# Filters made earlier and Strassen factors kept on chip in the first image, and the last projection shared out differently, in a YOLO-style attention block on one core

## The chip, the cores and the metric

The kernel runs on one core of a Trainium2 chip. The metric is device time in microseconds of one execution. Every run has a granted TensorE clock in its record (1.0 is full speed).

## The reference, cut to what matters

```python
B, C1, C2, N, F, HEADS = 8, 512, 512, 2, 32, 4     # 8 images of 32x32, C = 256, fp32
# per image (the tail is told in comments, the functions are the reference's own)
# y = cbs(x, cv1_w): 1x1, 512 -> 512, cut into two halves of 256 channels, y0 and y1
# for i in 0, 1:     3x3 convolution (256 -> 256) + silu, qkv 1x1,
#                    attention of 4 heads over 1024 positions, then m_cv2 (1x1),
#                    silu, plus the residual -> y2, y3
# out = cbs(concat(y0, y1, y2, y3), cv2_w) + x
def cbs(x, w, p, pad):
    return jax.nn.silu(bn_eval(conv2d(x, w, pad), p))

def bot_attention(x, qkv_w, rw, rh):
    ...
    r = (rw + rh).reshape(1, HEADS, HD, hw)
    logits = jnp.einsum('bhdi,bhdj->bhij', q, k + r) * HD ** (-0.5)
    a = jax.nn.softmax(logits, axis=-1)
    out = jnp.einsum('bhij,bhdj->bhdi', a, v)
```

## The kernel before

The kernel takes the images one after the other. Three of its devices matter here.

**Convolution by transformed filters.** A 3x3 convolution is done on transformed inputs and transformed filters (`u`), in three *pairs*. For image 0 VectorE makes the filters (`make_u`) from raw weights and stores each pair (1 MB) to memory; images 1 to 7 only load them. The ring that holds filters has five slots of 1 MB.

```python
    def make(n, oc, i):
        us[oc, i] = u = new_u("u_new")
        for k in range(NM):
            last = make_u(i, u[:, k], raws[n, oc, k])
        nc.gpsimd.dma_start(u_dram[n][oc][i], u)
        return last
...
        def u_of(n):
            def of(oc):
                if b == 0 and (oc, 0) not in us:     # second half of the channels, image 0
                    for k in range(NM):
                        if (n, oc, k) not in raws:
                            raws[n, oc, k] = load_raw(n, oc, k, "kv"[k])
                    with tc.issue_after(last.ins):
                        for i in range(PAIRS):
                            make(n, oc, i)
```

**Strassen for the last projection (cv2) of images 0 to 6.** Four sums of weight blocks are made once, in image 0, stored, and read back by every image, image 0 too. `make_ws` stores them, `load_ws` reads four half-MB sums and three source blocks. Image 7 uses plain products, with parts of them done early (`parts`, `begun`) so that its end is short.

**Attention in four groups** (two channel blocks by two halves of positions). While a group runs, the one before it is finished: a row of softmax sums goes to memory and comes back over 128 partitions, VectorE takes reciprocals (`rc`), which go to memory and back as a spread tile (`rs`), and `scale` multiplies. The accumulator of attention times V (`av_ps`) has one buffer; it is released by the add in `times_v`. An instruction on VectorE that waits holds up those queued behind it (shown below, L574 behind L640).

```python
                if j0 + PAIR == NJ:                 # times_v, last pair of a group
                    nc.scalar.copy(dst, av[:, 0])
                    nc.vector.tensor_tensor(dst, av[:, 1], dst, ALU.add)    # releases av_ps
...
            for i in range(len(pairs) + 1):
                if i < len(pairs):
                    added = logits(pairs[i])
                    g, at_q = divmod(i, NQ)
                    with tc.issue_after(added.ins):
                        if at_q == NQ - 2 and g > 0:
                            rss[g - 1] = spread(g - 1, s_drams[g - 1])     # rc, r_dram, rs
                        if at_q == 0 and g > 1:
                            scale(g - 2, rss.pop(g - 2))                   # waits for rs
```

The end of image 7 takes output pieces of 128 x 512 through two `t` buffers (add the early part, silu, add the residual `x_res`, store).

## Time and profile before

| | us |
|---|---|
| time before, median of the first three runs | 2406.1 |
| the profiled run (span; clock 0.995) | 2407.3 |
| image 0, from its first convolution to image 1's | 316.5 |
| ... its first attention / second convolution / second attention | 58.2 / 28.9 / 68.3 |
| images 1 to 6, each | 292.5 to 294.1 |
| image 7, last m2 (the 1x1 convolution after the attention) to the last add | 28.0 |

Stages are timed from the start of their first matmul on TensorE to that of the next stage; the second convolution is timed to the end of its last matmul, and qkv from there, since the two overlap by 0.16 us. The timeline of TensorE after the second convolution of image 0 (columns: start, length, engine, line, operation, output<-inputs; in brackets the idle time before it and who ended it, where there was any):

```profile
216.64 3.60 PE L303 MATMUL ps<-z,qkv_sb 128*128 128x512 f32 x8
220.07 1.03 PE L489 MATMUL v_ps<-qkv_sb,z 128*128 128x256 f32 x4
221.13 3.70 PE L303 MATMUL ps<-z,qkv_sb 128*128 128x512 f32 x8
```

And VectorE at the very end:

```profile
2398.14 1.35 DVE L928 TENSOR_TENSOR t<-ps,part 128x512 f32<-128x512 f32 x2 [3.90 <-PE ps L303]
```

VectorE waits 3.90 us for TensorE's products, so TensorE is what the end of the kernel before hangs on.

### The profile page before, as it was taken

The numbers are of one execution on the slowest core, as the hardware profiler recorded it, in microseconds if no ns is written. First come the engines' busy times: TensorE is split into PE (matmuls) and PEld (weight loads), VectorE is DVE, ScalarE is ACT, GpSimd is POOL, SyncE is SP. The second block draws the span as 40 slices with busy tenths as digits, with TensorE's granted clock in tenths as the row PEclk, the third lists the DMA queues.
The fourth block names the chain that finished last, engine by engine and source line by source line (L and its number), as shares of the span: only waits on it lengthen the run. The fifth ranks groups of instructions, "written<-read, shape, count | busy, mean of one in ns | idle before, by whom it ended". The sixth has DMA issues, their size and how long they took to land.

```text
span 2407.3 us, 35330 instructions
## 1 busy us (share of the span) xinstructions
PE 2358.4 (98%) x14514; PEld 1180.1 (49%) x14514; DVE 1589.4 (66%) x2549; ACT 925.7 (38%) x1230; POOL 85.6 (4%) x301
## 2 busy tenths in 40 slices
PE   7999899999999999999999999999999999999998
PEld 4536246363453635536364463645536364463633
DVE  8867675666766667666676656866566765666654
ACT  1442423526244251443425344252432525325252
POOL 1000000000100001000010000100001000000001
PEclk9999999999999999999999999999999999999999
DMA  7312325030340304203051021601107020150202
GB/s 244 116 34 97 132 78 207 15 114 15 114 167 15 114 15 168 117 10 114 22 217 62 28 96 32 260 13 66 59 28 262 11 99 25 47 199 15 71 10 68
DMA packets 90376, 215.19 MB, mean 89 GB/s; under 512 B 27616, under 2 KB 48288, under 8 KB 77664
## 3 DMA queue, kind: packets, MB, share of 16 engines
q1 hardware_dynamic: 79008, 165.15, 19.9%
q0 software_dynamic: 11200, 47.72, 5.1%
q8 instruction: 116, 1.90, 0.3%
q14 instruction: 52, 0.43, 0.1%
HBM read 180.85 MB, written 31.98 MB: 88 GB/s over the span
## 4 chain that ended last, share of the span: by engine, by line
PE 92%; DVE 4%; DMA 3%; ACT 0%; issue 0%; SPq 0%; POOL 0%; ACTq 0%; DVEq 0%
PE ps L303 20%; PE av_ps L550 18%; PE l_ps L524 18%; PE c_ps L740 12%; PE c L795 8%; PE c_new L795 6%; PE m_ps L761 5%; PE v_ps L489 5%; DMA u<-u 1%; PE s_ps L568 1%; PE s_ps L586 1%; DMA rs<-r_dram 0%; DMA s_dram<-s_row 0%; DVE acc L536 0%; DVE v_in L362 0%
## 5 line engine op out<-in xcount | busy, mean ns | idle before, releaser
L528 ACT ACTIVATE pt<-l_ps 128x1024 f32<-128x1024 f32 x512 | 494.9, 1023 | 309.7 <-PE l_ps L524 308.3
L536 DVE TENSOR_TENSOR acc<-acc,pt 128x1024 f32<-128x1024 f32 x384 | 469.5, 1223 | 122.8 <-ACT pt L528 99.1
L550 PE MATMUL av_ps<-pt,vT 64*64 64x512 f32 x4096 | 486.8, 593 | 3.7 <-DVE ao L558 3.7
L524 PE MATMUL l_ps<-q,kr 64*64 64x512 f32 x4096 | 484.8, 591 | 0.0
L740 PE MATMUL c_ps<-v_in,u 128*128 128x128 f32 x2688 | 304.3, 275 | 7.0 <-DVE v_in L362 4.0
L740 PEld LDWEIGHTS c_ps<-v_in,u 128*128 128x128 f32 x2688 | 303.0, 192 | 14.9 <-issue 9.4
L524 PEld LDWEIGHTS l_ps<-q,kr 64*64 64x64 f32 x4096 | 153.8, 133 | 279.9 <-issue 268.3
L550 PEld LDWEIGHTS av_ps<-pt,vT 64*64 64x64 f32 x4096 | 152.1, 133 | 281.1 <-issue 228.1
L303 PE MATMUL ps<-z,qkv_sb 128*128 128x512 f32 x512 | 229.3, 595 | 1.3 <-ACT z L289 0.9
L303 PE MATMUL ps<-x,w 128*128 128x512 f32 x512 | 227.0, 600 | 2.2 <-DVE x L439 2.2
L534 DVE TENSOR_TENSOR acc<-pt 128x1024 f32<-128x1024 f32 x64 | 78.4, 1225 | 134.7 <-ACT pt L528 134.7
L303 PEld LDWEIGHTS ps<-x,w 128*128 128x128 f32 x512 | 96.8, 192 | 130.3 <-issue 127.0
L477 DVE TENSOR_TENSOR kr<-ps,rw_sb 128x512 f32<-128x512 f32 x64 | 41.2, 686 | 176.5 <-PE ps L303 176.5
L303 PEld LDWEIGHTS ps<-z,qkv_sb 128*128 128x128 f32 x512 | 94.7, 190 | 108.1 <-issue 91.8
L795 PE MATMUL c_new<-t_in,ws 128*128 128x512 f32 x336 | 145.3, 592 | 0.0
L369 ACT COPY m<-c_ps 128x256 f32<-128x256 f32 x96 | 35.5, 369 | 234.9 <-PE c_ps L740 226.6
L489 PE MATMUL v_ps<-qkv_sb,z 128*128 128x256 f32 x512 | 115.7, 379 | 0.0
L761 PE MATMUL m_ps<-ao,m_sb 128*128 128x512 f32 x256 | 112.5, 592 | 0.0
L489 PEld LDWEIGHTS v_ps<-qkv_sb,z 128*128 128x128 f32 x512 | 97.3, 190 | 26.9 <-issue 15.3
L795 PEld LDWEIGHTS c_new<-t_in,ws 128*128 128x128 f32 x336 | 63.8, 190 | 80.4 <-issue 77.0
L289 ACT ACTIVATE m_kept<-m_kept,bh,sh 128x512 f32<-128x512 f32 x42 | 31.9, 806 | 146.0 <-DVE m_kept L879 86.3
L624 DVE TENSOR_TENSOR ao<-ao,rs 128x512 f32<-128x512 f32 x64 | 44.1, 689 | 63.3 <-DMA rs<-r_dram 62.8
(153 smaller groups left out, 2130.7 us busy)
## 6 DMA issues: line engine op xcount, KB each, us to landing
u<-u SPq DMA_DIRECT2D x84, 1024.0 KB
x<-in_x_dram SPq DMA_DIRECT2D x32, 512.0 KB
x_res<-in_x_dram POOLq DMA_DIRECT2D x28, 512.0 KB, 9.1
ws<-s SPq DMA_DIRECT2D x28, 512.0 KB
out_dram<-m_kept POOLq DMA_DIRECT2D x28, 512.0 KB, 7.5
w<-in_cv_w_dram SPq DMA_DIRECT2D x13, 1024.0 KB
u<-u_new POOLq DMA_DIRECT2D x12, 1024.0 KB, 5.9
rs<-r_dram SPq DMA_DIRECT2D x96, 128.0 KB
```

The costliest lines, as they stand in the source:

```text
L303: nc.tensor.matmul(ps[:, half, :], w_of(k), rhs_of(k, half), start=(k == begin), stop=(k == end))
L477: nc.vector.tensor_tensor(dst, img(ps[:, half, :]), rw, ALU.add)
L489: nc.tensor.matmul(ps[:, at, :], z[:, k, ts(j0 + at, P)], qkv_sb[:, n, k, 2 * C : 3 * C], start=(k == 0), stop=(k == NM - 1),)
L524: nc.tensor.matmul(ps[kh * HD : (kh + 1) * HD, hd, :], kr[r, c, o : o + HD], q[r, c, ts(half, HALF)], start=True, stop=True,)
L528: exp = nc.scalar.activation(pt[:, i], ps, AF.Exp, scale=SCALE)
L534: return nc.vector.tensor_tensor(accs[g], pt[:, 0], pt[:, 1], ALU.add)
L536: ins = nc.vector.tensor_tensor(accs[g], accs[g], pt[:, i], ALU.add)
L550: nc.tensor.matmul(avs[g][hd * HD : (hd + 1) * HD, kh, :], vT[r, j, o : o + HD], pt[r, i, hd, :], start=(j == 0), stop=(j == NJ - 1),)
L624: nc.vector.tensor_tensor(dst, dst, rs, ALU.mult)
L740: nc.tensor.matmul(ps[:, row, col, :], us[i][:, k, row, SLOT[col], :], vs[i][:, k, row, col, :], start=(k == 0), stop=(k == NM - 1),)
L761: nc.tensor.matmul(pss[oc][:, half, :], m2_sb[:, n, k, ts(oc, P)], ao[:, k, ts(half, HALF)], start=(k == 0), stop=(k == NM - 1),)
L795: nc.tensor.matmul(ps[:, o, :], w[:, k, ts(o, P)], rhs[part][:, c, :], start=(k == 0 and not onto), stop=(k == KB - 1), skip_group_check=onto,
```

## The change

Three parts. Part 1: in image 0 the Strassen sums that VectorE has just made are handed to Strassen where they lie, with the source blocks; they are stored for the other images, but not read back. Part 2: of the three filter pairs of the second convolution's second half, pair 2 is made in group 0 of the first attention (stored, dropped and loaded again) and pair 0 in groups 1 and 2 (kept); pair 1 alone stays beside the convolution. Part 3: image 7's early products are shared out differently: four more are begun in the gap before its last convolution, and the last block is ordered half by half.

```diff
 def make_ws(w2):
-        return [nc.gpsimd.dma_start(dst, w) for w, dst in zip(sums, s_dram2)][-1]
+        last = [nc.gpsimd.dma_start(dst, w) for w, dst in zip(sums, s_dram2)][-1]
+        return last, (a11, s1, a12, s4, s2, s3, a22)
 ...
-                three = s.strassen(b, load_ws(), y0, y1)
+                three = s.strassen(b, ws or load_ws(), y0, y1)
 ...                                                       # part 2
-                    with tc.issue_after(last.ins):
-                        for i in range(PAIRS):
-                            make(n, oc, i)
+                        with tc.issue_after(last.ins):
+                            make(n, oc, [1])
 ...
+            if b == 0:                                     # ahead(), first attention
+                if g == 0:
+                    raws[1, 1, 0], raws[1, 1, 1] = load_raws_y0(1, 1)
+                    make(1, 1, [2])
+                    del us[1, 2]
+                elif g <= NM:
+                    make(1, 1, [0], [g - 1])
 ...                                                       # part 3
-            for oc in range(3, NO):
-                parts[oc] = s.cv2_part(w1, (y0, y1), oc)
+            parts[3] = s.cv2_part(w1, (y0, y1), 3)
+            parts[0] = s.cv2_part(w1, (y0, y1), 0, range(NM))
 ...
-                begun = s.cv2_products(w2, (y0, y1, y2), 0, range(N * NM))
+                ks = range(NM, (1 + N) * NM)
+                begun[0] = s.cv2_products(w2, (y0, y1, y2), 0, ks, ends=(ks[0], (2 + N) * NM - 1))
 ...
-                s.cv2_products(w2, (y0, y1, y2), 0, range(N * NM, (1 + N) * NM), begun)
+                ks = range(2 * NM, (1 + N) * NM)
+                begun[1] = ps_av.tile([P, NH, HALF], F32, tag="av", name="ps")
+                s.cv2_products(w2, (y0, y1, y2), 1, ks, begun[1], (ks[0], (2 + N) * NM - 1))
 ...                                                       # in cv2(): the last block by halves
+                        ps = cv2_products(w2, ys, oc, ks, ends=(ks[0], ks[-1]), by_half=oc == NO - 1)
```

Left out: `make` in its form by pairs and channel groups, and the loading of raw filters in two tiles (`load_raws_y0`).

More of the change, by code (lines that the diff above doesn't have):

```diff
@@ L123, in load_w2, with rows_of_raw @@
         return ws
+    def rows_of_raw(raw):
+        rows = raw.rearrange("p (r c) o -> p r c o", c=3)
+        return rows[:, 0::2], rows[:, 1]
     def load_raw(n, oc, k, tag, bufs=1):
@@ L127, in load_raw, with load_raws_y0 @@
         nc.sync.dma_start(raw, m_cv1_w[n, ts(k, P), :, ts(oc, P)])
-        return raw
+        return rows_of_raw(raw)
+    def load_raws_y0(n, oc):
+        raw = act.tile([P, 16, P], F32, tag="y0", name="raw", bufs=2)
+        mid = act.tile([P, 3, P], F32, tag="xr", name="raw_mid", bufs=2)
+        src = m_cv1_w[n, P : 2 * P, :, ts(oc, P)].rearrange("p (r c) o -> p r c o", c=3)
+        both = raw[:, 9:15].rearrange("p (r c) o -> p r c o", c=3)
+        nc.sync.dma_start(raw[:, 0:9], m_cv1_w[n, ts(0, P), :, ts(oc, P)])
+        for r in range(2):
+            nc.sync.dma_start(both[:, r], src[:, 2 * r])
+        nc.sync.dma_start(mid, src[:, 1])
+        return rows_of_raw(raw[:, 0:9]), (both, mid)
     raws = {(0, 0, 0): load_raw(0, 0, 0, "k")}
@@ L241, in make_u @@
     def make_u(i, u, raw):
-        g0, g1, g2 = (raw[:, 3 * r : 3 * r + 3, :] for r in range(3))
+        rows, g1 = raw
+        g0, g2 = rows[:, 0], rows[:, 1]
         stt, tt = nc.vector.scalar_tensor_tensor, nc.vector.tensor_tensor
@@ L248, in make_u @@
         if i == 2:
-            rows = raw.rearrange("p (r c) o -> p r c o", c=3)[:, 0::2]
             nc.scalar.copy(u[:, :, 0:3:2], rows[:, :, 0::2])
@@ L293, in table_of, with conv1x1 @@
             nc.scalar.activation(spare, zero, func)
-        def conv1x1(w_of, rhs_of, nk, ks=None, ps=None, ends=None):
+        def conv1x1(w_of, rhs_of, nk, ks=None, ps=None, ends=None, by_half=False):
             if ps is None:
@@ L300, in conv1x1 @@
             begin, end = ends or (0, nk - 1)
-            for k in range(nk) if ks is None else ks:
-                for half in range(NH):
-                    nc.tensor.matmul(
-                        ps[:, half, :], w_of(k), rhs_of(k, half), start=(k == begin), stop=(k == end)
-                    )
+            ks = range(nk) if ks is None else ks
+            order = [(k, half) for k in ks for half in range(NH)]
+            for k, half in sorted(order, key=lambda a: a[1]) if by_half else order:
+                nc.tensor.matmul(ps[:, half, :], w_of(k), rhs_of(k, half), start=(k == begin), stop=(k == end))
             return ps
@@ L770, in m2, with cv2_products @@
             return last
-        def cv2_products(w2, ys, oc, ks, ps=None, ends=None):
+        def cv2_products(w2, ys, oc, ks, ps=None, ends=None, by_half=False):
             def cat(k, half):
@@ L779, in cv2_products @@
             nk = (2 + N) * NM
-            return conv1x1(lambda k: w2[2 * k // nk][:, k % (nk // 2), ts(oc, P)], cat, nk, ks, ps, ends)
+            return conv1x1(lambda k: w2[2 * k // nk][:, k % (nk // 2), ts(oc, P)], cat, nk, ks, ps, ends, by_half)
         def side(y, half):
@@ L888, in strassen, with cv2_part @@
             return part1, part2, part3
-        def cv2_part(w2, ys, oc):
-            ks = range(2 * NM)
+        def cv2_part(w2, ys, oc, ks=range(2 * NM)):
             ps = cv2_products(w2, ys, oc, ks, ends=(ks[0], ks[-1]))
@@ L897, in cv2_part, with cv2 @@
             return part
-        def cv2(b, w2, ys, begun=None, parts={}):
+        def cv2(b, w2, ys, begun={}, parts={}):
             def rows_of(dram, oc, half):
@@ L917, in cv2 @@
                     ks = range((2 + N) * NM)
-                    if oc in parts:
-                        ks = ks[2 * NM :]
-                        ps = cv2_products(w2, ys, oc, ks, ends=(ks[0], ks[-1]))
-                    elif i == 0 and begun is not None:
-                        ps = cv2_products(w2, ys, oc, ks[-NM:], begun)
-                    else:
-                        ps = cv2_products(w2, ys, oc, ks)
+                    if oc in begun:
+                        ps = cv2_products(w2, ys, oc, ks[-NM:], begun[oc], by_half=oc == NO - 1)
+                    else:
+                        ks = ks[2 * NM if oc in parts else 0 :]
+                        ps = cv2_products(w2, ys, oc, ks, ends=(ks[0], ks[-1]), by_half=oc == NO - 1)
                 t = act.tile([P, HALF], F32, tag="t", name="t", bufs=2)
@@ L949, with make @@
     us = {}
-    def make(n, oc, i):
-        us[oc, i] = u = new_u("u_new")
-        for k in range(NM):
-            last = make_u(i, u[:, k], raws[n, oc, k])
-        nc.gpsimd.dma_start(u_dram[n][oc][i], u)
+    def make(n, oc, pairs, ks=range(NM)):
+        for k in ks:
+            for i in pairs:
+                if k == 0:
+                    us[oc, i] = new_u("u_new")
+                last = make_u(i, us[oc, i][:, k], raws[n, oc, k])
+                if k == NM - 1:
+                    nc.gpsimd.dma_start(u_dram[n][oc][i], us[oc, i])
         return last
@@ L995, in of @@
             def of(oc):
-                if b == 0 and (oc, 0) not in us:
-                    for k in range(NM):
-                        if (n, oc, k) not in raws:
+                if b == 0 and oc == 1:
+                    if n == 0:
+                        with tc.issue_after(last.ins):
+                            for i in range(PAIRS):
+                                make(n, oc, [i])
+                    else:
+                        for k in range(NM):
                             raws[n, oc, k] = load_raw(n, oc, k, "kv"[k])
-                    with tc.issue_after(last.ins):
-                        for i in range(PAIRS):
-                            make(n, oc, i)
+                        with tc.issue_after(last.ins):
+                            make(n, oc, [1])
                 return [us.pop((oc, i)) if (oc, i) in us else load_u(n, oc, i) for i in range(PAIRS)]
@@ L1049 @@
         if b == 0:
-            behind[-1] = lambda: [make(1, 0, i) for i in range(PAIRS)]
+            behind[-1] = lambda: make(1, 0, range(PAIRS))
         ao, check = s.attention_fast(0, z, b * N * NM * NH, behind)
@@ L1063 @@
         z = s.conv3x3(1, vs, u_of(1))
-        w2 = begun = three = stored = None
+        w2 = ws = three = stored = None
+        begun = {}
         if b == 0:
@@ L1068, in prepare @@
         def prepare():
-            nonlocal stored
-            stored = make_ws(w2)
+            nonlocal stored, ws
+            stored, ws = make_ws(w2)
         def ahead():
@@ L1081, in first @@
         def first():
-            nonlocal begun
             if more:
```

## The prediction

> **What bounds the kernel now.** I read the page first, then TensorE's waits over the whole span, then tables of stretches, which set an image at the edge of the run beside one in the middle, and last each engine's order in time inside the stretches that came out long.
>
> ```profile
> PE 2358.4 (98%) x14514; PEld 1180.1 (49%) x14514; DVE 1589.4 (66%) x2549; ACT 925.7 (38%) x1230; POOL 85.6 (4%) x301
> ```
>
> TensorE is busy 2358.4 of 2407.3 us: a change that removes no matmul can win only some of the 49 us of gaps, and what a throttled clock adds around them. Who ends the gaps:
>
> ```profile
> PE s_ps L568 <- DVE acc L536: 4.7, 1, 4.7
> PE c_ps L740 <- DVE u_new L256: 4.3, 1, 4.3
> PE c_ps L740 <- DVE v_in L362: 4.0, 3, 1.6
> PE av_ps L550 <- DVE ao L558: 3.7, 3, 2.7
> ```
>
> All of these lie in the first and the last image. An image in the middle takes 292.5 us and loses 0.1 (the chain puts the starts of the first convolution at 949.64, 1242.11, 1535.17). Image 0 takes 316.5 us from its first convolution (46.19) to image 1's (362.69): 24 us too many. The same stages side by side:
>
> ```profile
> 94.00:152.40 58.40, 58.40 (x542) 20.21 (x542) 45.22 (x56) 36.05 (x43) 1.21 (x3) 1.00 0.05 16
> 237.70:306.00 68.30, 60.27 (x538) 20.05 (x537) 40.66 (x39) 36.12 (x42) 2.69 (x6) 0.93 0.33 120
> 543.10:600.50 57.40, 57.40 (x538) 19.76 (x537) 36.52 (x35) 36.02 (x42) 0.17 (x2) 1.00 0.05 15
> ```
>
> Columns: stretch, its length, busy us of PE, weight loads, DVE, ACT, POOL, then the granted clock. Image 0's second attention takes 68.3 us, image 1's 57.4: 8.0 us are gaps, the rest a clock of 0.93. And the second convolution, image 0 against image 1:
>
> ```profile
> 187.90:216.80 28.90, 24.30 (x194) 23.84 (x193) 28.14 (x77) 5.86 (x11) 1.83 (x5) 0.88 0.47 174
> 500.80:522.30 21.50, 21.50 (x194) 21.48 (x193) 17.51 (x48) 4.71 (x9) 0.18 (x2) 1.00 0.77 269
> ```
>
> 28.9 against 21.5 us, with VectorE busy 28.14 of 28.9: it is the bound there, since it makes the filters of the second half.
>
> The cause in the second attention is on the sync queue and VectorE:
>
> ```profile
> 219.18 29.30 SPq L148 DMA_DIRECT2D ws<-in_cv_w_dram  x2
> 259.85 0.56 SPq L575 DMA_DIRECT2D s_dram<-s_row  x1
> 272.11 0.20 DVE L612 RECIPROCAL rc<-sums_all 128x8 f32<-128x8 f32 x1 [9.02 <-DMA sums_all<-s_dram]
> 274.89 1.08 PE L568 MATMUL s_ps<-acc,ones 128*32 128x256 f32 x8 [4.67 <-DVE acc L536]
> 278.71 3.69 PE L550 MATMUL av_ps<-pt,vT 64*64 64x512 f32 x16 [2.74 <-DVE ao L558]
> ```
>
> A 4 KB transfer of softmax sums stands behind 3.5 MB of Strassen blocks and then shares the DMA engines with them: 10.72 us in the chain. VectorE, in order, waits 9.02 us for it, and TensorE 4.67 and 2.74 us for VectorE.
>
> **What the Trainium skill says.** "TensorE: Matmul & The Clock Gate", Part 1 (What's actually happening), says that an idle window of about 3.4 us halves the array's clock. The trace agrees where gaps are long: 0.50 at 274 to 280 us and 0.71 after it; gaps of 1.65, 1.25 and 1.06 us in the last image left it at 1.00, while two of 1.2 us near 62 us were followed by 0.72. [...]"DMA: Bandwidth & Descriptors", Issuing engines are not separate DMA queues, says that all issuers share 16 engines: the DMA share is 0.97 to 1.06 at 250 to 268 us, while both queues move blocks. "VectorE: DVE Perf Modes", the perf-mode tier table, gives fp32 tensor_tensor only its lowest rate; the trace has 1.22 us for 128x1024 and 0.33 to 0.34 us from start to start for 128x256. I take the durations from the trace.
>
> **Part 1: Strassen's factors stay on chip in image 0.** Four half-MB loads of sums and three of source blocks go (3.5 MB); the sums' stores (2.1 MB) stay. The new order of the sync queue has one filter load before the first sums transfer, where there were seven blocks and that load. VectorE's four sums (4.56 us) stay, so the later 0.63 us gap at 256 us stays. What is left should look like image 1's second attention: 57.3 + 0.6 = 57.9 us against 68.24 (237.74 to 305.98). Gain 10.3 us. Slots of the filter ring come free no later than before, so image 1's short wait for a filter (1.5 us) should stay; Strassen itself 0.3 us better, at most.
>
> **Part 2: two of the three filter pairs of the second half made in the first attention.** Per 128 channels, pair 0 costs VectorE three ops of 0.47 and three of 0.33 us (2.4 us), pair 2 three of 0.33 (1.0 us): for both channel groups 6.8 us leave the stretch at 187 to 217. Pair 1 (4.8 us) stays. I walked the new VectorE order with these durations: TensorE starts the second half at 198.8 instead of 203.3; pair 1's second group is complete only at 206.0, where its matmuls would want it at 202.4, but the new TensorE order runs 13 of pair 2's 16 matmuls in between, and pair 2 comes from memory, loaded since about 192 (1 MB, some 5 us). So the convolution ends near 209.5, not 216.8: 7.3 us, of which 4.6 are gaps and the rest throttled clock. A part is given back: pairs 1 and 2 now end together, so VectorE has two column passes (1.33 us each) and the rows' end after the last matmul. I get the first activated half at 5.9 us after it, where TensorE has other work for 4.3: a new wait of 1.6 us. Net 5.7 us.
>
> The moved work goes where VectorE is busy 45.2 of 58.4 us (first attention); 6.8 more makes 89%. It has only 3 to 4 us of slack in each of the four groups, and the groups that get it are those of the next image's statistics. Group 0: 2.0 us of pair 2 push the release of the attention accumulator (111.06) to 112.6, wanted at 111.97: 0.6 us. Group 1: 2.4 us ahead of the reciprocal move it from 119.3 to 122.6; the round trip from reciprocal to spread row takes 5.1 us (150.4 to 155.47 elsewhere in this trace), so the scaling waits till 127.8, the accumulator behind it in the queue is freed at 129.2, and TensorE wants it at 127.1: 2.1 us. Groups 2 and 3 absorb theirs. Loss 2.7 us. The extra raw loads (1 MB) fall at 80 to 90 us, where DMA is at most three quarters busy.
>
> **Part 3: last image.**
>
> ```profile
> 2236.00:2262.00 26.00, 22.04 (x100) 13.63 (x98) 18.54 (x43) 5.90 (x10) 0.68 (x8) 1.00 0.26 83
> 2373.00:2398.20 25.20, 24.61 (x59) 10.51 (x58) 10.62 (x20) 6.74 (x9) 6.42 (x12) 1.00 0.37 117
> ```
>
> Between m2 and its convolution TensorE idles 3.96 us behind VectorE's v_in, which ends at 2261.9 in any case. Four more 128x512 products (the trace counts each fp32 one twice, 0.43 us each pass, so 3.43 us) fit there free, and the final row has 24 instead of 28: 20.6 us for 24.0. The amounts after attention are the same (8 and 4). Working half by half on the last block ought to save 0.7 us more, but the new VectorE order puts that half's last add behind an add of the other half, so I count 0.3. Against it: every piece now passes two `t` buffers, each freed by an output store (3.0 us median to landing), and x_res takes 4.0 us; pieces come every 1.7 us at first, not 3.4, and the order now chains piece after piece. Walking that chain, the last add ends 25.3 us after m2 (28.0 before). Gain 2.7 us, not 3.7.
>
> **Sum.** 10.3 + 0.3 + 5.7 - 2.7 + 2.7 = 16.3 us; 2406.1 - 16.3 = 2389.8. Some small waits in my walk may be swallowed by three-deep buffers, so I say 2389.
>
> **The rivals.** (a) The moved filter work makes VectorE the bound of the first attention: groups of 13.8 us hold over 13 us of work, and each late accumulator stops TensorE; with a throttle after them this could cost 6 to 8 us and leave 2395. For it: slices at 100 to 106 and 112 to 118 us already show VectorE 5.86 of 6. Against: later groups have 4 us free. (b) The sums transfer is slow because of the stores, not the loads: 2.1 MB still move from 250 us on. Then some 3 us of part 1 stay, 2392. Against: stores need about 6 us at the 360 to 410 GB/s seen there, over by the time the sums are read. (c) Everything is hidden and neither the 1.6 nor the 2.7 us come: 2385. (d) The second half of the convolution waits for the reloaded pair 2, its store and load being in series: 3 us more. Against: the store was issued some 80 us earlier.
>
> **Range and chances.** The sum of ideal gains is 20.6 us (2385.5), the pessimistic waits add up to 2396 or 2397. Range 2382 to 2397. Over 2% faster would need 48 us, all the idle time there is; slower by 2% would need a new long stall, and nothing in the middle six images changes. Faster 0.01, within 2% 0.98, slower 0.01.
>
> **What would show it.** Second attention of image 0 near 58 us at clock 1.00, with no wait for DVE acc; the second convolution about 22 us plus a wait of ACT z on TensorE; the first attention 60 to 62 us, with a new wait on ao L574; the gap before the last convolution 0.5 to 1.1 us instead of 4; the last row 21 us of TensorE, and output adds waiting for stores. I am wrong if the first attention costs over 5 us, if the sums transfer still takes over 5 us, or if images 1 to 6 change by more than 1 us each.

## The result, and the profile after

The changed kernel took 2392.2 us (median of six runs, 2389.82 to 2394.27), the kernel before 2405.87 (six runs of the same rounds): ratio 0.994, with a 95% interval of 0.9927 to 0.9953. That is 13.7 us. A ratio here is the mean time of one kernel's runs over that of the other's runs of the same rounds, so it is not quite the ratio of the medians that are quoted.

The page's line of busy times, changed kernel:

```profile
PE 2352.9 (98%) x14514; PEld 1176.4 (49%) x14514; DVE 1589.9 (66%) x2551; ACT 927.2 (39%) x1232; POOL 86.0 (4%) x301
```

The same 14514 matmuls are 5.5 us shorter than before: that much of the gain is clock, the rest is gaps. The three stages of image 0 in the changed kernel, first attention, second convolution, second attention (columns as in the prediction):

```profile
93.20:155.80 62.60, 58.48 (x542) 20.09 (x541) 51.65 (x74) 36.02 (x42) 2.27 (x5) 1.00 0.15 55
191.40:213.00 21.60, 21.60 (x194) 21.55 (x193) 18.89 (x53) 4.83 (x9) 0.77 (x3) 1.00 0.53 188
237.70:295.70 58.00, 57.38 (x538) 19.68 (x537) 40.78 (x39) 36.02 (x42) 2.70 (x6) 1.00 0.20 68
```

The convolution has become 21.6 us of unbroken matmuls at full clock, and the second attention 58.0 us, image 1's 57.4 us plus one gap of 0.6 us. Both are what the change was for. But the first attention is now 62.6 us long with 58.48 us of matmuls in it: 4.1 us of new gaps. VectorE is busy 51.65 us there where it was 45.22.

Why the second attention is short: the sync queue of the changed kernel at the sums of its first group.

```profile
256.48 0.55 SPq L591 DMA_DIRECT2D s_dram<-s_row  x1
259.50 0.34 SPq L621 DMA_DIRECT2D sums_all<-s_dram  x1
```

The read is issued 3.0 us after the store of 4 KB, and can be only when the store has landed; in the kernel before, the profile's chain of work that ended last gave that store 10.72 us. Nothing stands before it on its queue now.

TensorE's timeline in the changed kernel, only its new gaps in image 0:

```profile
111.58 1.95 PE L566 MATMUL av_ps<-pt,vT 64*64 64x512 f32 x16 [0.48 <-DVE ao L574]
...
128.18 1.95 PE L566 MATMUL av_ps<-pt,vT 64*64 64x512 f32 x16 [2.06 <-DVE ao L574]
...
144.76 1.95 PE L566 MATMUL av_ps<-pt,vT 64*64 64x512 f32 x16 [1.57 <-DVE ao L574]
...
217.13 1.10 PE L505 MATMUL v_ps<-qkv_sb,z 128*128 128x256 f32 x4 [0.62 <-DVE r_ends L389]
219.41 5.40 PE L321 MATMUL ps<-z,qkv_sb 128*128 128x512 f32 x8 [1.17 <-ACT z L306]
```

The first three are the starts of groups 1 to 3 of the first attention, each held by the release of the accumulator: 4.1 us. The last two are qkv after the convolution: 1.8 us of waits where there were none, and then eight passes in 5.40 us which took 3.70 before. Nothing in the code explains those 1.7 us; it is the clock (0.72 between 219 and 225 us).

VectorE around the second and third of these gaps:

```profile
121.53 0.20 DVE L628 RECIPROCAL rc<-sums_all 128x8 f32<-128x8 f32 x1
...
126.83 0.69 DVE L640 TENSOR_TENSOR ao<-ao,rs 128x512 f32<-128x512 f32 x1 [1.43 <-DMA rs<-r_dram]
127.44 0.68 DVE L574 TENSOR_TENSOR ao<-av_ps,ao 128x512 f32<-128x512 f32 x1
...
136.27 0.20 DVE L628 RECIPROCAL rc<-sums_all 128x8 f32<-128x8 f32 x1
...
143.41 0.69 DVE L640 TENSOR_TENSOR ao<-ao,rs 128x512 f32<-128x512 f32 x1 [1.82 <-DMA rs<-r_dram]
144.02 0.68 DVE L574 TENSOR_TENSOR ao<-av_ps,ao 128x512 f32<-128x512 f32 x1
```

The scaling (L640) waits idle for the spread reciprocals, and the release (L574), which needs none of them, stands behind it in the queue. VectorE is not short of time here: it idles while TensorE waits for it. In the kernel before, whose first attention started 0.9 us later, the two reciprocals ran at 119.26 and 133.24 us, and the scaling had its data when its turn came.

The end, VectorE of the changed kernel:

```profile
2373.10 0.69 DVE L941 TENSOR_TENSOR t<-ps,part 128x512 f32<-128x512 f32 x1 [2.03 <-DMA out_dram<-t]
...
2385.79 0.69 DVE L941 TENSOR_TENSOR t<-ps,part 128x512 f32<-128x512 f32 x1 [1.55 <-DMA out_dram<-t]
...
2387.36 0.69 DVE L944 TENSOR_TENSOR t<-t,x_res 128x512 f32<-128x512 f32 x1 [0.28 <-ACT t L306]
```

Before, the adds waited for TensorE; now they wait for stores that free `t`. The last add ends 25.3 us after m2 (28.0 before).

Where the time went, by stage, for the two profiled runs:

| stage of image 0 | before | after |
|---|---|---|
| first convolution to first attention | 47.99 | 46.35 |
| first attention | 58.23 | 62.57 |
| to the second convolution | 35.66 | 35.65 |
| second convolution | 28.90 | 21.73 |
| qkv after it | 20.87 | 24.57 |
| second attention | 68.30 | 57.98 |
| Strassen and what follows, to image 1 | 56.56 | 56.25 |
| image 0 in all | 316.51 | 305.10 |

Images 1 to 6 took 1758.9 and 1759.1 us: untouched. (In the twelve later traces they took 1755.3 to 1757.9 us, though no edit aims at them. So up to 4 us of the difference between two runs can come from there, which is why single parts are read by stage.) The first row is odd, since the change does nothing there; it comes back below.

### The profile page after: what moved, and what is told of

Its sections match the earlier page's. It is cut to its first block, busy times and chain, and to the rows that moved or that the text cites. A ratio compares the mean times of both kernels' runs of the same rounds, so it can differ in the third digit from the quotient of the medians.

```text
span 2392.7 us, 35333 instructions
## 1 busy us (share of the span) xinstructions
PE 2352.9 (98%) x14514; PEld 1176.4 (49%) x14514; DVE 1589.9 (66%) x2551; ACT 927.2 (39%) x1232; POOL 86.0 (4%) x301
## 4 chain that ended last, share of the span: by engine, by line
PE 93%; DVE 4%; DMA 1%; ACT 1%; issue 0%; SPq 0%; POOL 0%; DVEq 0%; ACTq 0%
PE ps L321 20%; PE av_ps L566 17%; PE l_ps L540 17%; PE c_ps L756 13%; PE c L811 8%; PE c_new L811 6%; PE m_ps L777 5%; PE v_ps L505 5%; DVE acc L552 1%; PE s_ps L584 1%; PE s_ps L602 1%; DMA rs<-r_dram 0%; DVE st L421 0%; DMA x<-in_x_dram 0%; DMA r_dram<-rc 0%
## 5 line engine op out<-in xcount | busy, mean ns | idle before, releaser
L811 PE MATMUL c_new<-t_in,ws 128*128 128x512 f32 x288 | 124.6, 592 | 0.0
L811 PEld LDWEIGHTS c_new<-t_in,ws 128*128 128x128 f32 x288 | 54.7, 190 | 68.9 <-issue 66.0
L640 DVE TENSOR_TENSOR ao<-ao,rs 128x512 f32<-128x512 f32 x64 | 44.1, 688 | 63.4 <-DMA rs<-r_dram 62.8
```

The costliest lines, as they stand in the source:

```text
L640: nc.vector.tensor_tensor(dst, dst, rs, ALU.mult)
L811: nc.tensor.matmul(ps[:, o, :], w[:, k, ts(o, P)], rhs[part][:, c, :], start=(k == 0 and not onto), stop=(k == KB - 1), skip_group_check=onto,
```

## The experiments

Twelve runs, all with the right result: eleven kernels, and the changed kernel once more. Medians of the kernel before in the three sets were 2406.8, 2406.85 and 2406.0 us.

My theory after reading the two traces: parts 1 and 3 bring what was predicted and add up; part 2 gains its 7.3 us at the convolution and gives nearly all of it back, because the filter work delays the reciprocals and the release of the accumulator is queued behind the scaling, and because the convolution's ends now come late. The main rival: VectorE simply has too much to do in the first attention.

**Each part by itself.** First, part 1 alone on the kernel before:

```diff
-        return [nc.gpsimd.dma_start(dst, w) for w, dst in zip(sums, s_dram2)][-1]
+        last = [nc.gpsimd.dma_start(dst, w) for w, dst in zip(sums, s_dram2)][-1]
+        return last, (a11, s1, a12, s4, s2, s3, a22)
...
-                three = s.strassen(b, load_ws(), y0, y1)
+                three = s.strassen(b, ws or load_ws(), y0, y1)
```

> Part 1 alone on the kernel before. Theory (the stretches of the two traces add up): second attention of image 0 falls from 68.2 to about 58 us, nothing else moves, so 10.3 to 10.8 us less than the kernel before, about 2395.5. Rival (the parts help each other, part 1 needs the shorter convolution ahead of it): the sums' landing stays over 5 us, gain 6 us or less, about 2400.

Measured: 2396.69 us (2393.85 to 2397.81), ratio 0.996 (0.9947 to 0.9974), so 10.1 us less by the medians. The stretch of its second attention:

```profile
236.50:294.60 58.10, 57.46 (x538) 19.66 (x536) 40.79 (x39) 36.02 (x42) 2.70 (x6) 1.00 0.20 67
```

58.07 us for 68.30, clock 1.00. Image 0 takes 305.91 us, 10.6 less: 10.2 of it here, 0.2 in Strassen and 0.2 in the second convolution. The stores are still made, and the sums are read 2.9 us after their own store is issued, so the stores are not what made the sums slow. The rival falls. Whether the 3.5 MB of loads slowed the sums by standing before them on the queue or by sharing the DMA engines, no run tells apart.

Part 2 alone (the edit is the middle part of the diff above):

> Part 2 alone. Theory (after the result): the convolution gains 7.3 us and the first attention, the wait after the convolution and its throttled clock give 7 to 8 back, so 0 us, within 1 us of the kernel before, about 2406. Rival (the prediction's sum for this part, 7.3 - 1.6 - 2.7): 3.0 us faster, 2403. Note that the second attention still waits for the sums behind the reloaded blocks here, and the earlier end of the convolution could be swallowed there or not.

Measured: 2405.51 us (2403.66 to 2407.68), ratio 0.9997 (0.9983 to 1.0011). The interval spans 4 us faster to 3 us slower, so the medians exclude neither expectation. By stages: first attention +4.36, convolution -7.18, qkv after it +3.71, second attention -1.0 (67.29 us, with the slow sums still in it), Strassen -0.3, and the first row of the table -1.6, which is not the change's doing. In all 2.05 us less. Leaving out what the clock did by chance (the 1.6 us, and 1.7 of the 3.71), the sum is 2.1 us less.

Part 3 alone (the last part of the diff):

> Part 3 alone. Prediction's term: 2.7 us faster, 2403.2, last add 25.3 us after m2. Rival from the trace after: also the 1.5 us between the last add and the end of the span belong to it, so 4.2 us faster, 2401.7.

Measured: 2403.65 us (2402.76 to 2404.72), ratio 0.9988 (0.9974 to 1.0001), 3.2 us less by the medians. The last add ends 25.4 us after m2, 2.6 us earlier than before; from there to the end of the span it took 5.6 us. Over all the traces that last stretch was between 4.7 and 6.2 us (6.2, 6.0 and 5.4 in the three with the old ending), so the 1.5 us by which it differed between the first two traces is scatter. The rival of 4.2 us falls, the predicted 2.7 stands.

And the changed kernel without part 2:

```diff
-                            make(n, oc, [1])
+                            for i in range(PAIRS):
+                                make(n, oc, [i])
...
-            if b == 0:
-                if g == 0:
-                    raws[1, 1, 0], raws[1, 1, 1] = load_raws_y0(1, 1)
-                    ...
```

> The changed kernel without part 2. Theory (part 2 nets nothing): same time as the changed kernel within 1 us, 2391.5 to 2393, with image 0's second convolution at 28.5 us again and its first attention at 58.3. Rival (part 2 is worth the 3.0 us of the prediction, and the traces' starts mislead by noise): 3 us slower than the changed kernel, 2395.

Measured: 2393.45 us (2392.56 to 2394.24), ratio 0.9945, 1.3 us more than the changed kernel (2392.2, and 2392.08 in a later set). It lies between the two expectations. First attention 58.23, convolution 29.03, qkv 20.86 us: all three back to before. The times exclude neither expectation: against the kernel before in its own set, this kernel saves 13.4 us and the changed kernel 13.7, a difference far inside the scatter. By the stages of the two traces, part 2 beside parts 1 and 3 costs 0.4 us (first attention +4.3, convolution -7.3, qkv +3.7, Strassen -0.3, the first row left out); where the clock holds after the convolution (qkv +2.0), it gains 1.3 us. So the stages are nearer to "nothing", my theory after the result, than to the three microseconds of the prediction. The three parts alone save 10.1, 1.3 and 3.2 us by the medians, 14.6 together, and 13.7 when they are all made: they add up within the scatter.

**The scaling behind the release.** What costs the first attention its 4.3 us?

```diff
-                        if at_q == 0 and g > 1:
+                        if at_q == 1 and g > 1:
                             scale(g - 2, rss.pop(g - 2))
```

> The changed kernel with one edit: in the first attentions the scaling of a finished group is put behind the release of the attention accumulator on VectorE, no longer ahead of it. Theory (the three waits of 0.48, 2.06 and 1.57 us for ao come from the scaling, which waits for the spread reciprocals, ahead of the release in VectorE's order): the three waits fall to at most 1.2 us together, first attention near 59.5 us, 3 us faster than the changed kernel, 2389. Rival (VectorE simply has too much work in these groups, rival (a) of the prediction): the waits stay at 3 to 4 us under another name, 0 to 1 us faster.

Measured: 2387.0 us (2384.34 to 2389.21), ratio 0.9916 (0.9902 to 0.9929), 5.2 us less than the changed kernel by the medians of the two sets. First attention 58.81 us for 62.57. VectorE has the same work in it, only in another order. TensorE's gaps in it are now a single one:

```profile
111.03 1.95 PE L566 MATMUL av_ps<-pt,vT 64*64 64x512 f32 x16 [0.49 <-DVE ao L574]
```

The waits of 2.06 and 1.57 us are gone, as the theory says; the rival (too much work) falls. What is left, 0.49 us, is the filter work of group 0, which stands before the release itself. The gain was larger than the 3 us expected: the two waits were 3.6 us of it in the trace, and another 1.7 us came from qkv after the convolution (22.87 us for 24.57), with the same two waits in it, but no throttled clock after them. The five runs' median shows the larger gain too; how much of that is clock, I can't tell, as only one run of five has a trace.

**The third pair early too.** What costs 3.7 us after the convolution? In this kernel pair 1 is made between the first attention and m2, pair 0 gives up its slot and is loaded again, and the convolution runs without any filter work.

```diff
                         for k in range(NM):
-                            raws[n, oc, k] = load_raw(n, oc, k, "kv"[k])
-                        with tc.issue_after(last.ins):
-                            make(n, oc, [1])
+                            pass
...
                     make(1, 1, [0], [g - 1])
+                    if g == NM:
+                        del us[1, 0]
...
+        if b == 0:                       # after attention_fast(0, ...), before m2
+            for k in range(NM):
+                raws[1, 1, k] = load_raw(1, 1, k, "kv"[k])
+            make(1, 1, [1])
```

> The changed kernel with the third filter pair too made ahead of the second convolution, in the 36 us between the first attention and it, so that VectorE makes no filter during it. Theory (the 3.8 us after the convolution come from the two pairs ending together, with all of VectorE's ends after the last matmul): the waits for r_ends and z are gone, clock 1.00 there, second attention starts about 3.8 us sooner, 2388.5. Rival (the ends are late anyway, and the new filter work delays m2 or its attention): at most 1 us faster, 2391 or more.

Measured: 2388.41 us (2387.48 to 2391.01), ratio 0.9924 (0.9911 to 0.9938), 3.8 us less than the changed kernel. TensorE after the convolution:

```profile
211.53 3.60 PE L321 MATMUL ps<-z,qkv_sb 128*128 128x512 f32 x8
214.97 1.03 PE L505 MATMUL v_ps<-qkv_sb,z 128*128 128x256 f32 x4
216.02 3.70 PE L321 MATMUL ps<-z,qkv_sb 128*128 128x512 f32 x8
```

Both waits and the throttled passes are gone; the stretch is 20.86 us, that of the kernel before, and the convolution still 21.60. The theory held in what it forecast, to the tenth: with pair 1's filter work gone from the convolution, nothing is late after it. The run does not tell apart the pairs' ending together from VectorE's being late with pair 1's filters; for the first speaks the changed kernel's trace, where VectorE's column passes for both pairs start only at 212.91 and 214.24 us, beside the end of the last matmul (213.08).

**Four buffers at the end.** Are the waits for stores in the last row worth anything?

```diff
-                t = act.tile([P, HALF], F32, tag="xr", name="x_res", bufs=2)
+                t = act.tile([P, HALF], F32, tag=("xr", "rs")[oc % 2], name="x_res", bufs=2)
...
-                t = act.tile([P, HALF], F32, tag="t", name="t", bufs=2)
+                t = act.tile([P, HALF], F32, tag=("t", "h")[oc % 2], name="t", bufs=2)
... (the first four residuals are loaded ahead, not two)
```

> The changed kernel with four output buffers and four residual buffers in the last image in place of two each. Theory (the last adds wait for stores to free buffers: 2.03, 0.55 and 1.55 us, and for x_res 1.27): the last add ends near 23.5 us after m2 in place of 25.3, 1.5 to 2 us faster, 2390.5. Rival (the last add follows TensorE's last product, and the waits are slack): under 0.5 us.

Measured: 2390.03 us (2388.84 to 2390.84), ratio 0.9927 (0.9913 to 0.994), 2.2 us less than the changed kernel. The last add ends 23.75 us after m2, not 25.34. VectorE at the end:

```profile
2380.41 1.29 DVE L941 TENSOR_TENSOR t<-ps,part 128x512 f32<-128x512 f32 x2 [3.90 <-PE ps L321]
...
2381.98 1.40 DVE L944 TENSOR_TENSOR t<-t,x_res 128x512 f32<-128x512 f32 x2 [0.23 <-ACT t L306]
```

It waits for TensorE again, as before the change: part 3 had moved the bound of the end from TensorE to the buffers, and 1.6 us of its gain lay behind them. The edit gives two more output buffers and two more residual buffers at once, so their shares are not known. One more thing is to be seen: both halves of the last block are added together (x2) after TensorE's last product, though the products are ordered half by half so that the first half could go ahead.

**The three edits together.**

> The three edits together. Theory (they touch three separate places): their gains add, 8 to 9 us less than the changed kernel, 2383.5. Rival (they share VectorE and the DMA engines in image 0): less than 5 us, 2387.5 or more.

Measured: 2383.77 us (2382.72 to 2384.71), ratio 0.9904 (0.9889 to 0.9919), 8.4 us less than the changed kernel; the expected sum was 8 to 9. By the medians the single gains (5.2, 3.8, 2.2) do not add up to it, they sum to 11.2. By the stages they do: 3.8 in the first attention, 3.8 in the second convolution and after it, 1.6 at the end, 9.2 in all. Part of the difference may be that the 1.7 us of clock after the convolution, which the trace with the later scaling did not lose by luck, cannot be won a second time. Image 0 takes 297.51 us, 5 us more than the shortest images in the middle. This beats both kernels.

**The store of pair 0 later.** The third wait was not in the prediction. In the changed kernel's chain the 4 KB store of group 2's reciprocals takes 3.40 us (1.40 in group 1), and the 1 MB store of filter pair 0 had been issued 2.58 us before it. I tried to move that store behind the attention:

```diff
-                if k == NM - 1:
+                if k == NM - 1 and (n, oc, i) != (1, 1, 0):
                     nc.gpsimd.dma_start(u_dram[n][oc][i], us[oc, i])
...
+        if b == 0:                       # after attention_fast(0, ...)
+            nc.gpsimd.dma_start(u_dram[1][1][0], us[1, 0])
```

> The changed kernel with one edit: the 1 MB store of filter pair 0 is issued after the first attention, no longer in its third group. Theory (the third wait for ao, 1.57 us, which the prediction did not foresee, comes from the 4 KB store of the reciprocals, 3.40 us beside this store in place of 1.4): that store lands in about 1.4 us again, the third wait is gone, the second stays at 2.0, first attention near 61.0 us in place of 62.6. Rival (the reciprocal of that group is late in any case, since filter work stands ahead of it): third wait stays over 1.2 us.

Measured: 2392.19 us (2391.26 to 2392.72), the third wait 1.63 us. It looks like a win for the rival, but the trace says that the edit did not do what it was made for. The DMA issues of GpSimd, then the sync queue, in this run:

```profile
133.76 0.53 POOL L1079 DMA_DIRECT2D u<-u_new  x1 [28.07 <-DVE dev L433]
```

```profile
136.34 0.33 SPq L630 DMA_DIRECT2D r_dram<-rc  x1
139.80 1.11 SPq L632 DMA_DIRECT2D rs<-r_dram  x2
```

The store, now written at line 1079, still went out at 133.76 us: the order is set by a scheduler, which issued it as soon as its data was there. The run tells nothing apart. The control below does better.

**The changed kernel again.**

> The changed kernel once more, unaltered, as a control on the same chip. Theory (whether a short gap is followed by a throttled clock is chance): its two short-gap places, before the first attention and after the second convolution, each come out in one of two lengths, 46.35 or 48.0 us, and 22.9 or 24.6 us, and need not repeat the earlier trace (46.35 and 24.57); the waits themselves repeat to 0.1 us. Rival (the throttle belongs to the kernel): again 46.35 and 24.57. Time 2391 to 2393.5.

Measured: 2392.08 us (2389.41 to 2392.78), ratio 0.9942. Its gaps in the first attention:

```profile
111.62 1.95 PE L566 MATMUL av_ps<-pt,vT 64*64 64x512 f32 x16 [0.48 <-DVE ao L574]
...
128.07 3.29 PE L566 MATMUL av_ps<-pt,vT 64*64 64x512 f32 x16 [1.92 <-DVE ao L574]
```

and its sync queue in group 2:

```profile
136.77 0.33 SPq L630 DMA_DIRECT2D r_dram<-rc  x1
138.20 2.12 SPq L632 DMA_DIRECT2D rs<-r_dram  x2
```

The same kernel, and the clock fell elsewhere: before the first attention 47.92 us where the first trace had 46.35, after the convolution 22.87 where it had 24.57, and in the attention 3.29 us for 16 passes which took 1.95. So where the clock falls is no property of the change, and the odd first row of the table is explained. Over all fourteen traces, the same two gaps of 1.26 and 1.21 us in the first convolution were followed by a lost 1.6 us in five and by nothing in nine; the two waits after the second convolution by a lost 1.7 us in three traces of seven that have them.

The clock records in the traces say what decides it. The clock is 0.50 in every throttled stretch, each lasts 3.41 us or two or three times that (the last one of a run ends with the run), and where a trace has several, their starts lie whole multiples of 3.41 us apart: a grid, which lies elsewhere in each run. Laid over TensorE's busy time from 20 us on, the grid parts the cases cleanly. Of the 9673 cells of this grid, over all fourteen traces, that began at full clock, the 31 in which TensorE idled 1.75 us or more were all followed by a throttled one, and the other 9642, which idled 1.74 us at most, never. In the kernel before, the cell from 61.60 to 65.01 us holds 2.02 us of the two gaps, and the clock falls at 65.01; in the changed kernel's first trace the grid cuts the gaps apart, the cell from 62.91 us on holds 1.47 us, and nothing follows. A throttled cell costs at most half of 3.41 us, 1.7 us. What is chance is where the grid lies.

One expectation of mine missed: I wrote that the waits would repeat to 0.1 us. The third wait is not there at all. The throttled clock of 128 us had put group 2's reciprocal store 2.96 us after the 1 MB store (issued at 133.81) instead of 2.58, and it landed in the usual 1.4 us; TensorE was 1.3 us later as well. The kernel with four end buffers shows the same: 3.50 us of throttled passes at that place, store 3.01 us after the other, landed in 1.4 us, no third wait. In the five traces at 2.58 us, among them the one with the failed edit, it took about 3.4 us, and in the three with the later scaling, at 2.38 us, 3.8 us: it landed some 6 us after the big store was issued in all eight.

The DMA packets in the traces show where that time went. These are two of the three queues of the changed kernel from the small store's issue to the read that follows it (packets, MB, share of the engines):

```profile
q1 hardware_dynamic: 144, 0.00, 2.6%
q8 instruction: 1, 0.02, 1.9%
```

q1 is the small store, and q8 one packet of 16 KB of the kind that the page calls "instruction". The last packet of the big store ends at 137.86 us. The instruction packet starts there and takes 1.01 us. Of the 144 packets of the small store, 135 are through by 137.76 us, and the last nine start at 138.86, as the instruction packet ends. The order is the same in all eight traces: the instruction packet starts within 0.01 us of the big store's end, and nine packets follow it. In the six traces where the small store took 1.4 us, the instruction packet came after all 144 (at 138.64 us against 137.80 in this control). So the small store was held up by an instruction packet that came out behind the 1 MB store. Of its extra 2.0 us, the nine packets account for about 1.2, the slower start for 0.2, and 0.6 between the last packet and the read stays unexplained. Whether the instruction packet alone would have met the small store, no run shows. TensorE's lateness of 1.3 us also helps against the third wait, and no run moved the store alone. So the store's part in the wait stays argued, not shown.

**The last block's order, and its accumulators.** The kernel with the order of before in the last block:

```diff
-                        ps = cv2_products(w2, ys, oc, ks, ends=(ks[0], ks[-1]), by_half=oc == NO - 1)
+                        ps = cv2_products(w2, ys, oc, ks, ends=(ks[0], ks[-1]))
```

> The changed kernel with the last block's products in the order of before, not half by half. Theory (the add of the last block's first half waits for the last product of the whole tile, 0.1 us before it starts in the trace, so working by half brings nothing): same time within 1 us and last add 25.3 us after m2 as with it. Rival (it brings the 0.3 us of the prediction or the ideal 0.7): last add 25.6 to 26.0 us after m2.

Measured: 2391.62 us (2390.57 to 2393.61), last add 25.7 us after m2. The time says that the order is worth nothing that can be measured. The last add fits the rival's figure, but kernels with the order had 25.2 to 25.6, and here the last add also waited 0.40 us for a residual that was late; it does not separate 0 from 0.3 us. So I gave the two halves an accumulator each, on top of the three edits:

```diff
+            if by_half:
+                ps = [ps, ps_big.tile([P, NH, HALF], F32, tag="big", name="ps")]
...
-                nc.tensor.matmul(ps[:, half, :], ...)
+                to = ps[half] if by_half else ps
+                nc.tensor.matmul(to[:, half, :], ...)
```

> The version with the three edits, and the last block's two halves in two accumulators of their own. Theory (the first half's add waited for a tile, not for its half): it starts about 3 us before the last product, the last add ends about 0.7 us sooner after m2 (23.1 in place of 23.8), about 2383.0 us. Rival (the wait was for something else, order on the engine or a counter): 23.8 us after m2, no change.

Measured: 2383.18 us (2382.56 to 2384.25), ratio 0.9907 (0.9891 to 0.9922), which is not to be told from the 2383.77 of the three edits. But the trace is clear. VectorE at the end:

```profile
2369.59 0.69 DVE L944 TENSOR_TENSOR t<-ps,part 128x512 f32<-128x512 f32 x1 [0.46 <-PE ps L324]
...
2373.02 0.69 DVE L944 TENSOR_TENSOR t<-ps,part 128x512 f32<-128x512 f32 x1 [1.17 <-PE ps L324]
...
2374.59 0.69 DVE L947 TENSOR_TENSOR t<-t,x_res 128x512 f32<-128x512 f32 x1 [0.83 <-ACT t L306]
```

The first half's add starts at 2369.59, 3.4 us before TensorE's last product ends (2372.98), and the last add ends 23.0 us after m2, for 23.76. With one accumulator for both halves the first add had waited for the last product of the other half.

| kernel | median us | less than before |
|---|---|---|
| part 1 / part 2 / part 3 alone | 2396.7 / 2405.5 / 2403.7 | 10.1 / 1.3 / 3.2 |
| changed kernel, without part 2 | 2393.5 | 13.4 |
| changed kernel | 2392.2 | 13.7 |
| + scaling later / pair 1 early / four end buffers | 2387.0 / 2388.4 / 2390.0 | 19.9 / 18.4 / 16.8 |
| + all three | 2383.8 | 23.1 |
| + an accumulator per half | 2383.2 | 22.8 |

("Less" is against the median of before in the same set, so its differences are not quite those between the medians, which come from sets whose before differs by up to 1 us.)

## Why the prediction was right, point by point

The range held: 2389 was said, 2392.2 came, within 2382 to 2397. The sum was 16.3 us and 13.7 came.

- **Part 1, 10.3 + 0.3 us: right.** 10.32 in the second attention and 0.31 in Strassen, in the traces before and after; 10.6 in image 0 with part 1 alone. Setting the stretch beside the same one of an undisturbed image was a good way to size it. Rival (b), the stores, falls: they still run, and the sums are read 3.0 us after their store is issued.
- **Part 2, the convolution, 7.3 us: right** (7.2 by stages). Rival (d), waiting for the reloaded pair 2, did not come.
- **Part 2, the wait after it, 1.6 us: right in kind, short in size.** Two waits of 0.62 and 1.17 us; the first, for an accumulator that VectorE frees late, was not foreseen. The stretch is 2.0 us longer when the clock holds, and 3.7 when it does not.
- **Part 2, the first attention, 2.7 us: the mechanism right, the term mis-sized.** The waits at the starts of groups 1 and 2 (for the work that the prediction calls groups 0 and 1) came as walked: 0.48 for 0.6, and 2.06 for 2.1. The step that failed is "Groups 2 and 3 absorb theirs": group 3's start waited 1.57 us too, so the stage lost 4.3 us. The walk rested on the 5.1 us of a quiet trip from reciprocal to spread row. In group 1 it took 5.3 us (121.53 to 126.83), in group 2 7.1 us (136.27 to 143.41), with a 1 MB store of the moved work in flight. The moved work brought that transfer with it, and I had counted VectorE's time and the loads, not the store. The packets show the reciprocals' store held up by an instruction packet behind the 1 MB store; that the wait would go without the big store is not shown. In all, part 2 was put at 3.0 us (5.7 less 2.7) and came, beside the other parts and by stages, to between -0.4 and 1.3.
- **Rival (a), VectorE as the bound, was named but is not what happened.** With the same work in another order the waits went. The wait was one of order, not of load.
- **Part 3, 2.7 us: right.** 2.7 us in the trace of the changed kernel, 2.6 alone. The "0.3 for half by half" inside it was not seen to be there: the add waited for the whole tile.
- **Images 1 to 6 unchanged:** 0.3 us in 1759.

The account closes: 16.3, less 1.6 for the third wait, less 0.4 for the longer stretch after the convolution, is 14.3 us; less up to 1.7 us when the clock falls after that stretch, 12.6. Between the two lies the measured 13.7. Of the clock the prediction had said that a long gap costs nearly twice itself. Its own figures give less: 7.4 us too many for 4.6 us of gaps in the second convolution (28.9 against 21.5), and 10.9 for 8.0 in the second attention (68.3 against 57.4). For the gaps of 1 to 2 us that this change makes and removes, no factor holds: "TensorE: Matmul & The Clock Gate", Part 1 (What's actually happening), calls the window free-running, and the control shows what follows from it, the same gaps costing 1.6 us more in one run than in the next.

## What to carry to other kernels

When work is moved into an engine's idle time, look not at how much idle time there is but at what stands behind the new work in that engine's queue, and put the instructions that release a buffer ahead of those that wait for a transfer: one moved line gave back more than the whole of part 2. Count the transfers that come with moved work as well as its instructions: here a 4 KB store that the next step waits for came right behind a 1 MB store, with an instruction packet between them, and took 3.4 us in place of 1.4. And after shortening one engine's part of an ending, look at what it waits for next: two more output and residual buffers took the 1.6 us that the change had uncovered, while splitting the order of products did not let the first half go ahead until the halves had accumulators of their own.

## What the Trainium skill lacked or had wrong

- "TensorE: Matmul & The Clock Gate", Part 1 (What's actually happening): it puts the throttle "after ≥1 idle window (~3.4µs)". Here it took less: 1.75 us of idle time in one 3.41 us cell of the grid was enough (31 cells of 31), and 1.74 us was not (9642 cells). So gaps of 1.26 and 1.21 us, 2.1 us apart, were followed by 1.6 us lost in five traces of fourteen, and one wait of 1.9 to 2.1 us by 1.3 to 1.6 us lost in two traces of seven.
- "DMA: Bandwidth & Descriptors", Issuing engines are not separate DMA queues: it says that transfers of all issuers interleave on the same engines. That section gives no price for a small transfer beside a large one. Here a 4 KB store of reciprocals landed in 1.4 us in quiet, and in 3.4 us where it was issued 2.58 us after a 1 MB store of another engine; the 4 KB store of sums took 1.6 us in quiet, and 10.72 us in the kernel before, behind 3.5 MB of loads on its own queue.
- No page that I found says that a kernel's own transfers can be held up by instruction packets: nine of the 144 packets of that store of reciprocals stood for about 1 us behind one of 16 KB, in eight traces of fourteen.
- No page that I found says that a reader of one half of an accumulator may wait for the products of its other half: in this kernel the first half's add started within 0.1 us after the end of the last product with one accumulator for both, and 3.4 us before it with two.
